# Routed experts of a mixture layer: weights copied to DRAM, fetched per slot by a register address, and used as the stationary operand

## The chip, the cores and the metric

The kernel runs on one core of one Trainium2 chip. The metric is device time in microseconds (us) of one execution. The kernel before has a median of 1341.43 us over 11 runs (1333.9 to 1348.31). One further execution was taken with the hardware profiler; all stage times and durations below come from it.

## The reference, cut to what matters

The model is one block with three residual layers over `x` of 2 x 2048 x 128, float32:

```python
x = x + 0.5 * ffn(layernorm(x))     # mixture of experts
x = x + attn(layernorm(x))          # a state-space (scan) layer
x = x + 0.5 * ffn(layernorm(x))     # the same mixture, same weights
```

The mixture, for each of the 4096 tokens (D = H = 128, E = 32 experts, 4 chosen of them, plus a shared expert of width 512):

```python
scores = softmax(flat @ router_w.T + router_bias)
topk_scores, topk_idx = top_k(scores, 4)              # then normalised to sum 1
h = silu(flat @ gate_w[e].T) * (flat @ up_w[e].T)     # for the chosen e
out = sum over chosen e of score_e * (h @ down_w[e].T)
out = out + (silu(flat @ sgate_w.T) * (flat @ sup_w.T)) @ sdown_w.T
```

The scan layer has 256 channels with 16 states each; the state runs along the 2048 positions of a sequence.

## The kernel before, in words

The 4096 tokens are eight blocks of 512 tokens (4 tiles of 128). A mixture layer treats blocks in groups: the first layer has groups (0,1), (2,3), (4,5,6,7), the second (0,1,2,3), (4,5), (6,7). For one group, `mixture` does this:

1. LayerNorm, transposition and routing (mostly VectorE). The routing gives each (token, expert) pair a row in a DRAM buffer in which every expert's rows start on a tile of 128, and a list `route["sl"]` of the expert that owns each tile, or *slot*. A group of two blocks has 64 slots, one of four has 96.
2. GpSimd (POOL) scatters the tokens to their rows by indirect DMA, 128 rows at a time (L924, one for each tile and each of the 4 choices). The buffer has been filled with zeros before by SyncE's DMAs (`clear_rows`, L480), since slots are padded: 16 transfers of 256 KB for a two-block group and 24 for a four-block group. The three buffers are reused by the second layer.
3. Four slots at a time (a *quad*; 224 / 4 = 56 a layer): SyncE loads the rows (L1014, tile `xs`), PE transposes them (L1023, `pt_x`), ACT copies them out of PSUM (L1026, `xT`); PE computes gate and up in one matmul per slot (L1040, `gu`), in which `xT` is the stationary operand and 256 columns of the expert's weights move; ACT takes the SiLU (L1059), VectorE multiplies (L1065, `h`); PE transposes `h` (L1023, `pt_h`), ACT copies it (L1073, `hT`); PE computes the down projection (L1078, `oq`), ACT copies it (L1087, `yq`), SyncE stores it (L1091).
4. When all quads of the group are stored, POOL gathers, for each tile, the 4 results of its tokens by indirect DMA (L1105, `yg`), and PE adds them with diagonal matrices of the scores (L1130, `sum`).

The shared expert (L958, L967, L973, L984) is done by block. All weights of the 32 routed and 4 shared pieces lie in SBUF, in `w_all`, 55 KB of each partition; `load_experts` fills it with 27 transfers of 256 KB (L449). The expert of a slot is chosen by a register: PE loads four entries of `route["sl"]` (L1032) and uses them as column offsets into `w_flat`:

```python
nc.tensor.matmul(gu.t[:, s, :], xT.t[:, s0 + s, :],
                 w_flat[:, bass.ds(offs["v"][s0 + s], 2 * H)], start=True, stop=True)
```

The scan layer (`state_space`) takes the blocks one after another. In each of 16 state steps of a block, SyncE broadcasts a row (L1344, `bs`), POOL multiplies (L1354, the *drive*), ACT makes the decays (L1366, `da`), VectorE scans two channel halves (L1392) and multiplies by C (L1405), PE transposes and adds (L1171). Before its 16 steps a block has a prologue (projection, softplus; POOL's part at L1322 to L1324).

Every engine executes its instructions in order. That order is written out by hand: the kernel first collects 4504 operations, and `ORDER` lists their numbers in the order of emission; an operation goes to the end of its engine's queue, SyncE's too, whose queue holds all loads and stores but the indirect ones. Buffers come from rings (`RINGS`: name and depth); an operation that writes a ring's buffer waits until all users of the buffer that had its place are done. Between successive indirect DMAs POOL sets a small tile (L414, `pad`) as a pause.

Of the kernel before, what the change touches and what calls it, by code (L numbers as in the profile page):

```python
# [8 lines left out]
F32 = mybir.dt.float32  # L9
# [4 lines left out]
ALU = mybir.AluOpType  # L14
# [3 lines left out]
P = 128  # L18
# [22 lines left out]
    shb=1, sg=2, hs=4, xs=3, xT=2, h=2, hT=2, yq=2, yg=2, dg=1,  # L41
    pro=1, u=1, z=1, xnTs=1, t2=4, dt=2, dtu=2, bs=3, cm=2, hst=4,
# [5 lines left out]
1 96 10 0 109 12 8 4-5 14 20 7 11 25 9 6 13 21 52 113 112 16 111 114-117 121-122 877 876 879 118-119 123-124 120  # L48
125-131 178 180 179 182-183 181 184-185 132 134 133 135-138 186-187 190 188-189 191-194 878 880 195 881 139 196-198
882 199 142 200 202 201 203-205 208 206 209 207 892 210 883 211 143 140 212 884 141 887 213 144-145 888-889 988-993  # L50
996 994-995 997 1000 998 1001 999 893 1002 894 1003 885 1004 39 18 26 22 17 24 19 15 98 27 29 28 23 40 46 34 2 94 3
73 79 72 93 85 35 48 32 104 59 31 45 44 63 110 88 82 77-78 49 102 494 56 92 84 886 1005 897 895-896 495 898-899 1006
1008 1007 1010-1011 1009 1012-1015 1018 1016 1019 1017 890 146 167 164 169 158 175 151 156 162 177 172-174 168 150
176 161 153 165 152 170 154 147-149 159 155 157 171 160 163 166 1020 900 1021-1022 496-497 891 901-902 498-499 903
1023 500 1024 1026 1025 1028-1030 904 906 1027 908 81 97 74-75 36 62 41 103 43 47 91 42 100 89 30 57 86 76 50 33 71
95 69 83 37 87 53 38 80 1031 905 907 909 108 214 90 105 228 242 70 51 68 215 442 216 106 66 256 1032-1033 1036 1034
1037 1035 1038-1039 910 912 1040 911 913-915 1041 217-220 229 221-223 230 224 243 916 244 231-232 225-226 233-235
257-258 917 236 245 237 246 238 247-248 259 249-250 260-261 239-240 270 64 58 61 227 241 60 67 284 65 298 251-252
262-264 560-562 271-272 253 563 920 265 254-255 266 273 276 285 274-275 277 286 267-268 278 921 279-280 287 290
# [263 lines left out]
def macaron_kernel(  # L323
# [110 lines left out]
    rb = load("rb", router_b.partition_broadcast(P), [P, E])  # L434


    w_all = const.tile([P, NE, 3 * H], F32, tag="w_all", name="w_all")
    w_flat = w_all.rearrange("p e f -> p (e f)")
    w_routed, w_shared = Buf(t=w_all), Buf(t=w_all)

# [1113 lines left out]
```

## Time and profile before

| | |
|---|---|
| median of 11 runs | 1341.43 us (1333.9 to 1348.31) |
| the profiled execution: its own time | 1337.09 us |
| its span, first to last instruction | 1335.3 us |
| mean granted TensorE clock | 0.921 |
| busy: PE / DVE / ACT / POOL | 1064.0 / 858.3 / 896.9 / 999.8 us |
| DMA traffic | 154.12 MB, mean 115 GB/s |

Milestones of that execution, by the starts of POOL's instructions: the first scatter at 28.0 us; the first scatter of the first layer's four-block group at 93.9; the first gather at 212.3; the first scan drive at 282.1; the last scan of block 3 ends at 596.5; the gathers of the four-block group from 588.2; the first drive of block 4 at 663.4; the last store of a quad at 1278.5; the last gather ends at 1327.2.

How to read it: busy time of an engine says little by itself, since each engine has to wait in its fixed order. What a change is worth in a stretch is read from the chain of work that ended last in that stretch, and from which engine's queue was never empty there. The chain's shares are in per cent of the stretch.

### The profile page before, as it was taken

The numbers are of one execution on the slowest core, as the hardware profiler recorded it, in microseconds if no ns is written. First come the engines' busy times: TensorE is split into PE (matmuls) and PEld (weight loads), VectorE is DVE, ScalarE is ACT, GpSimd is POOL, SyncE is SP. The second block draws the span as 40 slices with busy tenths as digits, with TensorE's granted clock in tenths as the row PEclk, the third lists the DMA queues.
The fourth block names the chain that finished last, engine by engine and source line by source line (L and its number), as shares of the span: only waits on it lengthen the run. The fifth ranks groups of instructions, "written<-read, shape, count | busy, mean of one in ns | idle before, by whom it ended". The sixth has DMA issues, their size and how long they took to land.

```text
span 1335.3 us, 19281 instructions
## 1 busy us (share of the span) xinstructions
PE 1064.0 (80%) x5842; PEld 804.3 (60%) x5842; DVE 858.3 (64%) x1567; ACT 896.9 (67%) x1704; POOL 999.8 (75%) x1108
## 2 busy tenths in 40 slices
PE   6899877878876887878776676788888888788875
PEld 3567556656655766766444453555667777567753
DVE  7576412279799998982599999998995434112211
ACT  4446333799897999976767576587986555456532
POOL 2838888887898546577888888896458468878776
PEclk9999998998997999996989787788999998989987
DMA  9955334444333425421122232222444433444432
GB/s 307 347 161 170 100 93 139 134 121 128 91 110 99 118 76 150 120 72 40 58 68 67 74 88 69 62 68 78 129 125 141 124 101 110 132 142 129 123 99 54
DMA packets 186726, 154.12 MB, mean 115 GB/s; under 512 B 17665, under 2 KB 154498, under 8 KB 186626
## 3 DMA queue, kind: packets, MB, share of 16 engines
q1 hardware_dynamic: 170242, 119.29, 30.6%
q0 software_dynamic: 16384, 33.59, 8.8%
q8 instruction: 51, 0.84, 0.3%
q14 instruction: 49, 0.40, 0.1%
HBM read 89.64 MB, written 63.18 MB: 114 GB/s over the span
## 4 chain that ended last, share of the span: by engine, by line
PE 31%; DVE 26%; POOL 16%; ACT 13%; issue 10%; DMA 2%; another core or an unknown queue 0%; POOLq 0%; DVEq 0%; SPq 0%; ACTq 0%
DVE hst L1392 12%; PE gu L1040 7%; POOL xs L924 6%; POOL yg L1105 5%; PE oq L1078 4%; DVE hst L1405 4%; POOL pad L414 4%; ACT L420 4%; PE sum L1130 3%; ACT da L1366 3%; PE pt_h L1023 2%; PE gp L958 2%; PE up L958 2%; PE pt_x L1023 2%; PE y L1171 2%
## 5 line engine op out<-in xcount | busy, mean ns | idle before, releaser
L1354 POOL TENSOR_TENSOR hst<-dtu,bs 128x1024 f32<-128x1024 f32 x128 | 302.9, 2376 | 122.6 <-ACT st L1417 33.6
L1105 POOL DMA_INDIRECT yg<-ys,idx x256 | 249.1, 973 | 101.6 <-issue 38.9
L1040 PE MATMUL gu<-w_all,xT 128*128 x896 | 240.9, 405 | 28.6 <-issue 13.1
L1392 DVE TENSOR_TENSOR_SCAN hst<-da,st,hst 128x512 f32<-128x512 f32 x192 | 237.8, 1269 | 13.4 <-ACT da L1366 9.3
L924 POOL DMA_INDIRECT xs<-xn,idx x192 | 189.1, 985 | 62.5 <-issue 33.2
L1065 DVE TENSOR_TENSOR h<-sgq,gu 128x256 f32<-128x256 f32 x224 | 89.5, 415 | 207.7 <-ACT sgq L1059 126.2
L1366 ACT ACTIVATE da<-dt,a 128x512 f32<-128x512 f32 x256 | 174.0, 691 | 60.5 <-DVE hst L1392 57.4
L1040 PEld LDWEIGHTS gu<-w_all,xT 128*128 128x128 f32 x896 | 165.9, 199 | 74.3 <-issue 26.0
L420 ACT ACT_TABLE_LOAD x148 | 189.9, 1283 | 3.4 <-PEq L1542 0.8
L1171 PEld LDWEIGHTS y<-ident,hst 128*128 128x128 f32 x1024 | 128.7, 151 | 69.2 <-issue 45.3
L1405 DVE TENSOR_TENSOR hst<-hst,c 128x1024 f32<-128x1024 f32 x128 | 156.1, 1220 | 12.7 <-PE c L1378 4.1
L1171 PE MATMUL y<-ident,hst 128*128 128x128 f32 x1024 | 141.8, 290 | 14.8 <-DVE hst L1405 11.6
L1078 PE MATMUL oq<-w_all,hT 128*128 x896 | 123.1, 282 | 13.1 <-ACT hT L1073 8.1
L414 POOL MEMSET pad<- 128x256 bf16 x402 | 132.3, 329 | 0.3
L1078 PEld LDWEIGHTS oq<-w_all,hT 128*128 128x128 f32 x896 | 113.3, 195 | 28.0 <-ACT hT L1073 13.0
L1059 ACT ACTIVATE sgq<-gu 128x256 f32<-128x256 f32 x224 | 81.7, 382 | 71.7 <-PE gu L1040 46.4
L1130 PE MATMUL sum<-yg,dg 128*128 128x128 f32 x512 | 85.3, 312 | 39.2 <-DMA yg<-ys,idx 26.3
L1122 ACT ACTIVATE dg<-ident,wk 128x128 f32<-128x128 f32 x256 | 81.5, 391 | 47.6 <-PE sum L1130 34.3
L1023 PE MATMUL pt_h<-ident,h 128*128 128x128 f32 x448 | 75.7, 289 | 45.1 <-DVE h L1065 30.0
L1130 PEld LDWEIGHTS sum<-yg,dg 128*128 128x128 f32 x512 | 75.9, 219 | 56.0 <-issue 32.3
L1087 ACT COPY yq<-oq 128x512 f32<-128x512 f32 x112 | 65.2, 584 | 63.9 <-PE pt_h L1023 18.0
L1378 PE MATMUL c<-cm,pick 128*128 128x512 bf16 x128 | 52.5, 410 | 58.4 <-DVE hst L1405 58.4
(151 smaller groups left out, 1720.1 us busy)
## 6 DMA issues: line engine op xcount, KB each, us to landing
bs<-bd SPq DMA_DIRECT2D x128, 256.0 KB
xs<-xs SPq DMA_DIRECT2D x112, 256.0 KB
ys<-yq SPq DMA_DIRECT2D x112, 256.0 KB
xs<-zero SPq DMA_DIRECT2D x56, 256.0 KB
yg<-ys,idx POOLq DMA_INDIRECT x256
xs<-xn,idx POOLq DMA_INDIRECT x192
x<-in_x SPq DMA_DIRECT2D x8, 256.0 KB
w_all<-in_up_w SPq DMA_DIRECT2D x8, 256.0 KB
```

Source lines behind the costliest of these rows:

```text
L414: pool(nc.gpsimd.memset(pad, 0.0))
L420: nc.scalar.preload_act_table_set(name)
L924: nc.gpsimd.indirect_dma_start(out=xs_b.t, out_offset=bass.IndirectOffsetOnAxis(ap=route["idx"][:, i * TB + t, k : k + 1], axis=0), in_=xn ...
L1040: nc.tensor.matmul(gu.t[:, s, :], xT.t[:, s0 + s, :], w_flat[:, bass.ds(offs["v"][s0 + s], 2 * H)], start=True, stop=True,)
L1078: nc.tensor.matmul(o.t[:, s, :], hT.t[:, s, :], w_flat[:, bass.ds(offs["v"][s] + 2 * H, D)], start=True, stop=True,)
L1105: nc.gpsimd.indirect_dma_start(out=yg.t[:, k, :], out_offset=None, in_=ys_b.t, in_offset=bass.IndirectOffsetOnAxis(ap=route["idx"][:, i * ...
L1130: nc.tensor.matmul(sm_.t, dg.t[:, k, :], yg.t[:, k, :], start=(k == 0), stop=(k == TOPK - 1),)
L1171: nc.tensor.matmul(y[:, t, k * P : (k + 1) * P], src[:, k, t * P : (t + 1) * P], ident.t, is_transpose=True, start=start and k == 0 and t ...
L1354: nc.gpsimd.tensor_tensor(h.t[:, :, 1:], dtu.t, bs.t.unsqueeze(1).to_broadcast([P, ND, T]), ALU.mult)
L1366: nc.scalar.activation(da.t, dt.t[:, k, :], AF.Exp, scale=a_t.t[:, k, s : s + 1])
L1392: nc.vector.tensor_tensor_scan(h.t[:, k, 1:], da.t, h.t[:, k, 1:], 0.0 if ini else st_sb[:, k, s : s + 1], ALU.mult, ALU.add,)
L1405: nc.vector.tensor_tensor(h.t[:, :, :T], h.t[:, :, 1:], cb.t.unsqueeze(1).to_broadcast([P, ND, T]), ALU.mult,)
```

## The change

- The routed experts' weights no longer lie in SBUF. `load_experts` copies them at the start from the three inputs into one DRAM tensor `w_dram` of [32 experts, 128, 384] (24 transfers of 256 KB, DRAM to DRAM). `w_all` keeps the four shared pieces alone.
- For every quad, SyncE loads the four owners from `route["sl"]` into registers and starts four transfers of 192 KB (128 rows of 1536 bytes), one for each slot, from `w_dram` at the register's address into a new ring `wt` (8 buffers of two slots). They stand in SyncE's queue among the other loads and stores. PE no longer loads registers.
- Gate and up become two matmuls per slot with the weights stationary and `xT` moving (128 columns), so that `gu` comes out with H on the partitions. `h` then has the layout that the down projection wants, and the transposition `pt_h` and the copy `hT` are gone. The down projection takes its moving operand from `wt`.
- Rings: `sg` 2 to 3, `xs` 3 to 4, `xT` and `h` 2 to 3, `yq` 2 to 3, `yg` 2 to 4, `dg` 1 to 2, `u`, `z` and `xnTs` 1 to 2.
- `ORDER` is another list of the same length. On a coarse scale (stages, scan blocks against groups) it is the old one; on a fine scale most operations have moved.

```diff
 RINGS = dict(
     y=1, da=2, c=1, w=3,
     xn=4, xnT=3, rt=1, lo=1, sc=1, mr=1, mk=1, cum=1, sm=1, route=3,
-    shb=1, sg=2, hs=4, xs=3, xT=2, h=2, hT=2, yq=2, yg=2, dg=1,
-    pro=1, u=1, z=1, xnTs=1, t2=4, dt=2, dtu=2, bs=3, cm=2, hst=4,
+    shb=1, sg=3, hs=4, xs=4, xT=3, h=3, wt=8, yq=3, yg=4, dg=2,
+    pro=1, u=2, z=2, xnTs=2, t2=4, dt=2, dtu=2, bs=3, cm=2, hst=4,
 )
...
-    w_all = const.tile([P, NE, 3 * H], F32, tag="w_all", name="w_all")
-    w_flat = w_all.rearrange("p e f -> p (e f)")
-    w_routed, w_shared = Buf(t=w_all), Buf(t=w_all)
+    w_all = const.tile([P, NSH, 3 * H], F32, tag="w_all", name="w_all")
+    w_shared, w_routed = Buf(t=w_all), dram_buf("w_dram", [E, P, 3 * H])

     def load_experts(c):
         for j, srcs in enumerate(((gate_w, sgate_w), (up_w, sup_w), (down_w, sdown_w))):
             shared = c == E // ECH
-            src = srcs[1] if shared else srcs[0][:, c * ECH : (c + 1) * ECH, :]
-            dst = w_all[:, c * ECH : (c + 1) * ECH, j * H : (j + 1) * H]
+            es, hs = slice(c * ECH, (c + 1) * ECH), slice(j * H, (j + 1) * H)
+            src = srcs[1] if shared else srcs[0][:, es, :].rearrange("p e h -> e p h")
+            dst = w_all[:, :, hs] if shared else w_routed.t[es, :, hs]
...
-            nc.vector.tensor_scalar(ej, ej, float(E - 1), 3.0 * H, ALU.min, ALU.mult)
+            nc.vector.tensor_scalar(ej, ej, float(E - 1), None, ALU.min)
...
+            wts = []
+            for s0 in range(0, SQ, 2):
+                wt = buf("wt", [P, 2, 3 * H])
+
+                def fetch(q=q, s0=s0, wt=wt, offs=offs):
+                    if s0 == 0:
+                        _, offs["v"] = nc.values_load_multi_w_load_instructions(
+                            route["sl"][0:1, q * SQ : (q + 1) * SQ],
+                            engines=[ET.SP],
...
+                    for s in range(2):
+                        nc.sync.dma_start(
+                            wt.t[:, s, :],
+                            w_routed.t[bass.ds(offs["v"][s0 + s], 1)].rearrange("e p f -> p (e f)"),
+                        )
+
+                op("sp", 1.6, fetch, r=[sl_b, route_b, w_routed], w=[wt, offs_b], size=4 * P * 2 * 3 * H)
+                wts.append(wt)
...
-                    for s in range(2):
-                        nc.tensor.matmul(
-                            gu.t[:, s, :],
-                            xT.t[:, s0 + s, :],
-                            w_flat[:, bass.ds(offs["v"][s0 + s], 2 * H)],
...
+                def gate_up(s0=s0, gu=gu, xT=xT, wt=wt):
+                    for j in range(2):
+                        for s in range(2):
+                            nc.tensor.matmul(
+                                gu.t[:, j, s, :],
+                                wt.t[:, s, j * H : (j + 1) * H],
+                                xT.t[:, s0 + s, :],
+                                start=True,
+                                stop=True,
+                            )
...
-            ph = buf("w", [P, SQ, P], name="pt_h")
-            op("pe", 0.45, lambda turn=turn, a=ph, b=h: turn(a, b), r=[h], w=[ph], hold=[hT])
-            op("act", 0.49, lambda a=hT, b=ph: nc.scalar.copy(a.t, b.t), r=[ph], w=[hT])
...
-                        hT.t[:, s, :],
-                        w_flat[:, bass.ds(offs["v"][s] + 2 * H, D)],
+                        h.t[:, s, :],
+                        wts[s // 2].t[:, s % 2, 2 * H :],
```

## The prediction

> **What bounds the kernel now.** I read the page first (busy times, slices, DMA), then the chain of waits cut into stretches, then the waits of POOL and the durations of the lines that the change touches. The busy times name no single bound, and the slices show DMA full only at the start:
>
> ```profile
> PE 1064.0 (80%) x5842; PEld 804.3 (60%) x5842; DVE 858.3 (64%) x1567; ACT 896.9 (67%) x1704; POOL 999.8 (75%) x1108
> DMA  9955334444333425421122232222444433444432
> q1 hardware_dynamic: 170242, 119.29, 30.6%
> ```
>
> The chain, cut at 28, 262, 600, 650, 1010 and 1280 us, has another owner in each stretch. These are the answers for 28 to 262, 650 to 1010, 1010 to 1280 and the end:
>
> ```profile
> by line: POOL xs L924 32.9%; POOL pad L414 14.1%; issue 9.9%; POOL yg L1105 8.2%; PE o L984 6.1%; PE gp L958 5.6%; PE up L958 4.6%; DMA yg<-ys,idx 3.9%; DVE hs L973 1.5%; PE pt_n L644 1.4%; PE lg L691 1.4%; DVE mr L744 1.1%; DVE x L996 1.1%
> by line: DVE hst L1392 25.2%; issue 10.6%; DVE hst L1405 8.5%; PE y L1171 3.1%; ACT L420 3.1%; ACT da L1366 2.8%; PE gp L958 2.8%; PE ps L1193 2.7%; PE up L958 2.3%; DVE hs L973 2.2%; DVE ea L1308 2.2%; PE gu L1040 1.7%; DVE bc L1255 1.5%;
> by line: PE gu L1040 28.5%; PE oq L1078 14.7%; PE sum L1130 9.3%; issue 9.2%; PE pt_h L1023 8.1%; PE pt_x L1023 7.0%; DVE h L1065 2.7%; ACT yq L1087 2.2%; PE ps_o L1475 1.9%; PE y L1171 1.8%; ACT dg L1122 1.8%; ACT sgq L1059 1.6%; another c
> by line: POOL yg L1105 50.8%; POOL pad L414 18.0%; issue 8.1%; DMA out_y<-x 4.9%; DMA yg<-ys,idx 4.5%; PE sum L1130 2.9%; POOLq L1550 1.9%; POOLq L1105 1.1%; DVE x L1141 0.5%
> ```
>
> So POOL's indirect DMAs set the time up to the first scan drive, VectorE (with ACT in 262 to 600, busy 307.87 of 338 us) that of the scans, PE that of the last mixture, and POOL's 32 last gathers the end. POOL's two long waits matter most here:
>
> ```profile
> 27.95 1.13 POOL L924 DMA_INDIRECT xs<-xn,idx  x1 [24.95 <-DMA w_all<-in_up_w]
> 93.92 0.96 POOL L924 DMA_INDIRECT xs<-dtu,idx  x1 [18.84 <-ACT sgq L1059]
> 95.38 0.96 POOL L924 DMA_INDIRECT xs<-dtu,idx  x1 [0.16 <-issue]
> ```
>
> The first scatter waits for its zeroed rows (DMA). At 93.92 POOL begins the four-block group, held by the routing. From there indirect DMAs follow each other every 1.455 us with nothing between, up to the first drive at 282.1: POOL has no slack, and a later start moves everything behind it.
>
> **Part 1, the start: the copy into `w_dram`.** Before, 27 weight loads share the queue with the zero fills, 68 us of it at 300 to 350 GB/s, and the first `xs` load is issued at 76.0. After, 24 of them are copies inside DRAM whose source is written expert by expert: the slowest dimension has 4 entries, the destination has 512 rows. What does a transfer with few outer entries do? The trace has one: `bout`, a single row. From section 6, the packets of q1 that carry data are 136705 of 512 B (`xs` and `ys` 224 x 512, `w_all` 27 x 512, `x` and `out` 16 x 512, `bout` 1), 23936 of 2 KB (`bs` and the fills 184 x 128, `win`, `wdt`, `bd` 384) and 1984 smaller, 162625 together. The line above counts 170242; the 7617 left are 476 x 16 + 1, for 477 transfers. [...]
>
> q1 took 30.6% of 16 x 1335.3 us for 119.29 MB, 55 ns per KB, 28 ns per 512 B. A copy of 512 rows is 512 x 28 / 16 = 0.9 us on sixteen engines, or 128 x 28 ns = 3.6 us on four; 24 of them 21.5 or 86 us. Ahead of or between them the same engines serve 43 fills and 11 loads of 256 KB (0.76 us each at the 347 GB/s of the second slice, 41 us) and the first 32 scatters (about 5 us). So `w_dram` is complete at about 2 + 41 + 5 + 21.5 = 70 us, or at 134 us. I take four, because the only row of a transfer with fewer than 16 outer entries used that many engines and no more.
>
> [...]
>
> Who waits? SyncE's queue is in order. In the new listing the first fetch, which needs the whole of `w_dram`, stands right behind these copies, and behind it the first `xs` loads and the last zero fill of the four-block buffer, with 14 fetches in front. That fill is issued about 10 us after `w_dram` is complete (14 fetches at 0.36 to 0.45 us, five register loads, some fills) and lands some 5 us later, behind 14 x 192 KB. The scatter of 93.92 then starts at about 150, 56 us late. From it to the first drive the old list has 121 indirect DMAs, the new one 114: 7 x 1.455 = 10 us less. Net +46 us. Bounds: with sixteen engines the fill lands at about 85 to 95, no delay, and -10 remains; with four engines and slower rows inside DRAM (a third more, 29 us) +75. PE's first quad moves from 80 to about 143, and needs 78 us of PE work until the 16th is stored; the first gather stands 69 DMAs, 100 us, behind the scatter, so this hides, with some 20 us to spare.
>
> **Part 2, the quad.** Removed on PE: four transpositions, 0.47 us a quad in steady rows; the register load and four offsets (0.33 + 4 x 0.04 us), of which only 'issue' gaps show, 13 + 26 us in all. Added: gate and up take 8 matmuls of 128 columns instead of 4 of 256. Rows: `gu` x8 takes 1.71 us (4 slots), `oq` x8, 128 columns, 0.97; so 1.94 instead of 1.71. Net -0.24 us for each of 112 quads, -27 us of PE work. On ACT `hT` goes, 112 x 0.585 = 65 us, and 8 of 148 table loads of 1.28. SiLU and product keep shape and duration, 0. POOL loses 22 of 402 pauses.
>
> Added to SyncE, a quad: one register load, four offsets, four transfers (0.36 to 0.45 us each): about 2.2 us, 245 us in all, beside some 200 of now 477 transfers. [...] `wt` waits make `bs`, `xs` and `ys` transfers wait behind them, and POOL and PE for those. DMA gains 448 x 192 KB, 88 MB: by 55 ns per KB 0.66 us of all engines each, 2.6 a quad.
>
> By stretch, against 1337.1 us:
> - 262 to 600, 32 quads: ACT loses 19 us of 308, and about 30% of this chain is ACT; PE's `pt_h` and ACT's `hT` are 10 us of it. -12 (0 to -25).
> - 600 to 650: the new list puts 51 gathers instead of 42 before block 4's first drive: +13 (0 to +13). They are missing later among the drives of blocks 4 to 6, where VectorE is as near to the bound as POOL: -6 (0 to -13).
> - Last block, with `u`, `z`, `xnTs` doubled so that a prologue can go ahead: -5 (0 to -15); what is late next is VectorE, 337 of 360 us busy.
> - From the last scan to the last store, PE: the list has 164.5 us of PE work there before, 149.7 after, and the register gaps (8 us there): -17 (-35 to +10). Next is POOL, about 188 us of DMAs in the 255.
> - The 32 last gathers: 0.
> - SyncE's order and a fuller DMA queue: +5 (0 to +40), near the low end since `xs` waits cost PE 8.6 us in the whole run.
>
> Sum: 46 - 12 + 13 - 6 - 5 - 17 + 5 = +24, so 1361 us beside the profiled execution's 1337.1, which lies 0.32% under the median of 1341.43. For a median that is 1365 us.
>
> **The rivals.**
> - *Wide copy, faster.* The copies run on 16 engines. Place: the wait at 93.92. Then part 1 is -10 and the sum -32: 1305, as a median 1309. It decides from where the copy takes under some 1.3 us (no delay at all) and breaks even near 2.7 us (`w_dram` at about 113). For it: every transfer but one in the trace is wide. Against: the one that isn't.
> - *Queue behind the fetch.* The delay as forecast, and SyncE's waits for a `wt` buffer hold up `bs` loads and stores in the later stretches too; with +40 instead of +5, 1396, as a median 1400. For it: SyncE already waits 332 us for POOL's drives in front of `bs`; against: it is mostly early.
> - *Delay eaten.* As forecast at the start, but ACT and PE relief count fully (-25, -35, -13, -15, no gather cost): about 1295 + 46 = 1341 or less, no change.
> - That rings are deeper without effect where the list doesn't use them is part of the ranges above.
>
> **How the numbers follow.** Forecast 0.58, wide copy 0.15, queue 0.13, eaten 0.14. About 0.3% (4 us) is what a measurement here can tell from no change. Faster: 0.14 of the wide copy, 0.08 of the eaten delay, 0.03 of the forecast, 0.25. Same: 0.01 + 0.03 + 0.05 = 0.09. Slower: 0.66. The forecast's own range is 1340 to 1390. The 8-in-10 range reaches to the wide copy's 1309 with 6 us below, and to the queue's 1400: 1303 to 1402.
>
> **What would show it.** Right: DMA's slices fall to about a quarter (4 of 16 engines) before some 135 us, POOL's wait before the first `xs<-dtu` scatter grows from 18.8 to about 70 us and is ended by a fill, PE idles there, the first drive is near 328; the PE stretch before the last store is shorter by some 15 us; `pt_h` and `hT` rows are gone. Wrong: a first scatter of that group before 100 us (wide copy), or a first drive near 328 and a total beyond 1390 with SyncE's waits at `wt` ahead of `bs` (queue).

## The result and the profile after

The changed kernel takes 1396.13 us (median of 16 runs, 1389.31 to 1400.34), the kernel before 1339.5 us beside it (62 runs). The ratio is 1.0429, 95% interval 1.0411 to 1.0447: 57 us slower. The profiled execution took 1396.81 us, with a span of 1395.0 and a mean granted clock of 0.88.

The page of the kernel after, its lines for PE, the DMA slices and the first queue:

```profile
PE 1043.2 (75%) x6290; PEld 837.5 (60%) x6290; DVE 853.5 (61%) x1567; ACT 828.1 (59%) x1584; POOL 992.2 (71%) x1086
...
DMA  8547766876673567683112223224498867778841
...
q1 hardware_dynamic: 234466, 207.40, 48.8%
```

PE's busy time fell by 21 us (1064.0 to 1043.2), although it now runs 448 instructions more. The first queue carries 207.40 MB instead of 119.29. DMA's slices mostly stand at 5 to 8 where they were 2 to 5, in the first half of the span and again from the 29th slice on; in the ten slices between, the later scan blocks, they are 1 to 4 in both.

The windows view cuts both spans at the first scan drive and at the end of the last one. Its columns are the stretch, its length in us, busy us and count of PE, PEld, DVE, ACT and POOL, the clock, DMA's share and GB/s. Before:

```profile
0.00:282.10 282.10, 232.50 (x1204) 166.29 (x1205) 127.36 (x448) 141.76 (x284) 210.36 (x328) 0.97 0.57 176
282.10:1024.60 742.50, 582.38 (x3170) 435.72 (x3168) 646.57 (x878) 597.87 (x1056) 559.27 (x422) 0.90 0.33 93
1024.60:1335.30 310.70, 249.11 (x1471) 202.26 (x1470) 84.34 (x243) 157.32 (x365) 230.22 (x358) 0.93 0.41 114
```

After:

```profile
0.00:342.30 342.30, 242.55 (x1311) 183.82 (x1312) 124.52 (x444) 126.86 (x258) 198.63 (x313) 0.85 0.66 208
342.30:1087.00 744.70, 569.51 (x3436) 450.79 (x3436) 652.90 (x897) 576.16 (x1021) 587.25 (x453) 0.89 0.49 147
1087.00:1395.00 308.00, 231.09 (x1547) 202.91 (x1546) 76.09 (x228) 125.05 (x306) 206.29 (x321) 0.89 0.68 201
```

The first stretch grew by 60 us (282.1 to 342.3), the scans by 2 us, the last stretch shrank by 3. The whole loss lies ahead of the first drive. The scans and the last mixture have gained next to nothing.

The chain of waits after, for 28 to 342, 710 to 1065 and 1087 to 1338 (views cut short on the right by their width):

```profile
by line: issue 17.5%; PE gu L1061 11.0%; PE o L984 8.2%; PE oq L1089 6.9%; PE gp L958 6.3%; SPq L480 6.3%; PE up L958 6.1%; PE pt_x L1051 4.3%; SPq L449 3.8%; DVE h L1079 2.4%; PE lg L691 2.2%; DMA w_dram<-in_up_w 2.0%; PE sum L1141 1.8%; a
...
by line: DVE hst L1403 25.1%; ACT L419 9.2%; issue 8.5%; DVE hst L1416 6.5%; ACT da L1377 5.6%; PE y L1182 4.7%; PE o L984 2.7%; ACT sg L967 1.8%; PE ps_o L1486 1.7%; DVE ea L1319 1.5%; DVE hs L973 1.5%; DVE bc L1266 1.5%; POOL hst L1365 1.
...
by line: PE gu L1061 23.5%; issue 21.0%; PE oq L1089 14.6%; PE sum L1141 9.9%; PE pt_x L1051 8.0%; another core or an unknown queue 3.5%; DVE h L1079 2.9%; ACT sgq L1073 1.6%; ACT xT L1054 1.6%; PE ps_o L1486 1.5%; PE lg L691 1.5%; ACT xn L
```

At the start POOL's scatters (32.9% of 28 to 262 before) no longer own the chain: 'issue', PE's quads (`gu`, `oq`) and PE's shared expert (`o`, `gp`, `up`) do. The scans belong to VectorE as before. In the last mixture `pt_h` and `hT` are gone, but 'issue', time in which the engine waited for nothing that the profile shows, is 21.0% of 251 us, 53 us, where it was 9.2% of 270 us, 25 us. What was taken off PE did not come out of the stretch. The end is POOL's gathers as before (`yg` 45.0%, `pad` 16.0%).

POOL's five longest waits between 76 us and the first drive (POOL's timeline; start, duration, instruction, in brackets the idle time and its releaser):

```profile
141.92 0.96 POOL L924 DMA_INDIRECT xs<-dtu,idx  x1 [63.93 <-DMA wt<-w_dram]
...
197.85 0.96 POOL L924 DMA_INDIRECT xs<-xn,idx  x1 [12.21 <-DVE h L1079]
...
259.16 0.98 POOL L1116 DMA_INDIRECT yg<-ys,idx  x1 [4.71 <-DMA wt<-w_dram]
...
291.06 0.96 POOL L1116 DMA_INDIRECT yg<-ys,idx  x1 [2.75 <-PE sum L1141]
...
332.83 1.26 POOL L1333 TENSOR_TENSOR w<-w,ea 128x512 f32<-128x512 f32 x1 [7.05 <-ACT w L1328]
```

The wait of 18.84 us before the four-block group's first scatter became one of 63.93 us. Four more follow, 26.7 us together, the last of them before the scan's prologue; the kernel before has one of 1.22 us there.

**Who held the scatter at 141.92?** The releaser named there, a fetch, had nothing to do with its data. The timelines of PE, VectorE and SyncE give the answer. After:

```profile
130.41 1.09 PE L1051 MATMUL pt_x<-ident,xs 128*128 128x128 f32 x4 [34.83 <-DMA xs<-xs]
131.29 0.63 PE L769 MATMUL tot<-mk,ones 128*128 128x512 bf16 x1
```

```profile
91.75 1.25 DVE L757 TENSOR_SCALAR mk<-mr 128x512 bf16<-128x512 f32 x1
...
131.97 1.22 DVE L777 TENSOR_TENSOR_SCAN cum<-one,tot 128x512 f32<-128x512 f32 x1 [35.59 <-PE tot L769]
...
140.98 0.20 DVE L855 TENSOR_SCALAR idx<-p 128x64 uint32<-128x64 f32 x1
```

```profile
122.27 3.35 SPq L1033 DMA_DIRECT2D wt<-w_dram  x6
125.71 0.39 SPq L1014 DMA_DIRECT2D xs<-xs  x1
```

Before, PE and VectorE at the same place:

```profile
79.27 0.63 PE L1023 MATMUL pt_x<-ident,xs 128*128 128x128 f32 x4 [0.17 <-DMA xs<-xs]
```

```profile
84.04 1.21 DVE L777 TENSOR_TENSOR_SCAN cum<-one,tot 128x512 f32<-128x512 f32 x1
```

The scatter needs `idx`, the routing, which VectorE finished at 141.18. That chain begins with PE's matmul `tot` (L769). Its operand `mk` was ready at 93.00, 38 us before it ran; but in PE's queue `tot` stands right behind `pt_x`, the transposition of the first quad's rows, and PE idled 34.83 us until those rows came. Their load stands in SyncE's queue behind six fetches (issued from 122.27), which need the whole of `w_dram`. In the old list, too, `tot` comes behind the first `pt_x`, but there the rows were in time. From `cum` (L777) to the scatter it takes 9.95 us here and 9.88 before (84.04 to 93.92): only the beginning moved, by 47.9 us. In each of the 20 traces of this case the scatter starts 0.94 or 0.95 us after `idx` does.

### The profile page after: what moved, and what is told of

Its sections match the earlier page's. It is cut to its first block, busy times and chain, and to the rows that moved or that the text cites. A ratio compares the mean times of both kernels' runs of the same rounds, so it can differ in the third digit from the quotient of the medians.

```text
span 1395.0 us, 20723 instructions
## 1 busy us (share of the span) xinstructions
PE 1043.2 (75%) x6290; PEld 837.5 (60%) x6290; DVE 853.5 (61%) x1567; ACT 828.1 (59%) x1584; POOL 992.2 (71%) x1086
## 2 busy tenths in 40 slices
DMA packets 250961, 242.32 MB, mean 174 GB/s; under 512 B 24545, under 2 KB 218722, under 8 KB 250850
## 3 DMA queue, kind: packets, MB, share of 16 engines
q1 hardware_dynamic: 234466, 207.40, 48.8%
## 4 chain that ended last, share of the span: by engine, by line
PE 36%; DVE 27%; issue 14%; ACT 12%; POOL 5%; SPq 3%; DMA 2%; another core or an unknown queue 1%; POOLq 0%; DVEq 0%; ACTq 0%
DVE hst L1403 12%; PE gu L1061 8%; PE oq L1089 6%; ACT L419 3%; DVE hst L1416 3%; PE y L1182 3%; PE sum L1141 3%; PE pt_x L1051 3%; PE o L984 3%; POOL yg L1116 2%; ACT da L1377 2%; PE gp L958 2%; DVE h L1079 2%; PE up L958 2%; SPq L480 2%
## 5 line engine op out<-in xcount | busy, mean ns | idle before, releaser
L1061 PE MATMUL gu<-xT,wt 128*128 128x128 f32 x1792 | 248.8, 292 | 51.0 <-issue 21.1
L1061 PEld LDWEIGHTS gu<-xT,wt 128*128 128x128 f32 x1792 | 230.5, 204 | 78.8 <-issue 32.6
L1089 PE MATMUL oq<-wt,h 128*128 128x128 f32 x896 | 141.4, 308 | 43.6 <-DVE h L1079 26.6
L1089 PEld LDWEIGHTS oq<-wt,h 128*128 128x128 f32 x896 | 127.7, 218 | 56.4 <-DVE h L1079 31.8
L413 POOL MEMSET pad<- 128x256 bf16 x380 | 124.6, 328 | 0.2
L1051 PE MATMUL pt_x<-ident,xs 128*128 128x128 f32 x448 | 74.8, 299 | 65.6 <-DMA xs<-xs 38.8
L1054 ACT COPY xT<-pt_x 128x512 f32<-128x512 f32 x112 | 64.5, 584 | 90.6 <-PE pt_x L1051 66.1
L924 POOL DMA_INDIRECT xs<-dtu,idx x64 | 62.7, 979 | 75.4 <-DMA wt<-w_dram 63.9
L1051 PEld LDWEIGHTS pt_x<-ident,xs 128*128 128x128 f32 x448 | 57.4, 154 | 80.2 <-issue 62.4
L1141 PE MATMUL sum<-yg,dg 128*128 128x128 f32 x512 | 82.0, 313 | 29.8 <-DMA yg<-ys,idx 16.4
```

Source lines behind the costliest of these rows:

```text
L413: pool(nc.gpsimd.memset(pad, 0.0))
L924: nc.gpsimd.indirect_dma_start(out=xs_b.t, out_offset=bass.IndirectOffsetOnAxis(ap=route["idx"][:, i * TB + t, k : k + 1], axis=0), in_=xn ...
L1051: nc.tensor.transpose(dst_.t[:, s, :], src_.t[:, s, :], ident.t)
L1061: nc.tensor.matmul(gu.t[:, j, s, :], wt.t[:, s, j * H : (j + 1) * H], xT.t[:, s0 + s, :], start=True, stop=True,)
L1089: nc.tensor.matmul(o.t[:, s, :], h.t[:, s, :], wts[s // 2].t[:, s % 2, 2 * H :], start=True, stop=True,)
```

## Experiments

Times differ between occasions: the kernel before took 1397.5 us beside the first four runs below, 1338.5 to 1344.9 beside most others and 1321.9 once. So each run is read as its ratio to the kernel before on the same chip at the same time; stretches are from each run's profiled execution, cut as above. "Start" is the time of the first drive, "last" what follows the last drive.

### The copy: how wide, and whether at all

**The copy row by row.** The outer dimension of source and destination has 128 entries; nothing else differs.

```diff
-            src = srcs[1] if shared else srcs[0][:, es, :].rearrange("p e h -> e p h")
-            dst = w_all[:, :, hs] if shared else w_routed.t[es, :, hs]
+            src = srcs[1] if shared else srcs[0][:, es, :]
+            dst = w_all[:, :, hs] if shared else w_routed.t[es, :, hs].rearrange("e p h -> p e h")
```

> The changed kernel with one edit: the 24 copies into w_dram are written row by row on both sides (128 outer entries) instead of expert by expert (4). Same bytes, same queue, same order. Theory N (the narrow copy is the loss): w_dram is complete near 70 to 75 us, the first xs<-dtu scatter is at 85 to 100 us instead of 141.9, the first drive at 275 to 290 instead of 342.3, and as the two kernels take the same time from the first drive to the end (1052.7 and 1053.2 us) the total is 1330 to 1345. Theory Q (SyncE's order is the loss: fills and xs loads stand behind fetches, however fast the copy): the scatter stays beyond 110 us, total 1360 to 1385. Theory T (fetch traffic costs the later stages and the early delay was partly hidden): first drive near 282, but more than 1060 us from it to the end, total 1350 or more.

Measured: 1.0216 (1.0139 to 1.0294), the four-block scatter at 109.7, the first drive at 338.4. Less is lost than with the narrow copy, but neither scatter nor drive came as early as the first theory had them.

**No copy.** The weights come packed, as one input; `load_experts` loads the shared pieces alone.

```diff
...
-    w_shared, w_routed = Buf(t=w_all), dram_buf("w_dram", [E, P, 3 * H])
+    w_shared, w_routed = Buf(t=w_all), Buf(t=experts)
...
```

> The changed kernel without the copy: the host hands the experts' weights over already packed expert by expert (an arrangement of the same values), the fetches read that input, and the 24 copies are gone from SyncE and the DMA queue. Theory N: at least as early as the wide copy, by 0 to 20 us: scatter at 75 to 95 us, first drive 265 to 285, total 1320 to 1340. Theory Q: the scatter waits for the routing that the first fetch needs, and stays beyond 105 us, total 1355 to 1380. Theory T: first drive at 282 or before and still a total of 1345 or more.

Measured: 1.0101 (1.0031 to 1.0170), scatter at 99.1, first drive at 321.2, again later than expected.

**Zero fills first.** Nine fills of the four-block buffer move ahead of the first fetch in `ORDER`; the narrow copy stays.

> The changed kernel, narrow copy kept, with the nine zero fills that stood behind the first fetch on SyncE moved in front of it. Theory Q: the wait for the fill was the loss: scatter of the four-block group at 95 to 105 us, first drive at 290 to 300, total 1345 to 1355. Theory N with a second hold (the first quads start only when w_dram is complete near 120 us, and the in-order queues of VectorE and PE put them ahead of later routing): the scatter comes at about 95 to 105 us, but POOL waits later, for the routing and for the first ys rows, the first drive stays at 325 to 342, total 1378 to 1396.

Measured: 1.0495 (1.0405 to 1.0586), scatter at 147.1; both theories had it at 95 to 105. The fills were not what it waited for. Up to them the two SyncE queues agree within 0.5 us, though the chips differ: the last group of fills starts at 116.53 after and at 117.01 here. Behind it the first `xs` load is issued at 131.74 instead of 125.71, since the nine fills now stand ahead of it, and VectorE's timeline has the routing as much later:

```profile
131.74 0.39 SPq L1022 DMA_DIRECT2D xs<-xs  x1
```

```profile
137.40 1.22 DVE L785 TENSOR_TENSOR_SCAN cum<-one,tot 128x512 f32<-128x512 f32 x1 [33.38 <-PE tot L777]
...
146.17 0.20 DVE L863 TENSOR_SCALAR idx<-p 128x64 uint32<-128x64 f32 x1
```

Load +6.0, `cum` +5.4, `idx` +5.2, scatter +5.2 us: the chain through `pt_x` and `tot` carries the delay.

**Twelve copies of eight experts.** Each has eight outer entries.

```diff
+            whole = shared or c % 2
+            if not shared:
+                es = slice((c - 1) * ECH, (c + 1) * ECH)
+                src = srcs[0][:, es, :].rearrange("p e h -> e p h") if whole else None
+                dst = w_routed.t[es, :, hs] if whole else None
...
```

> The changed kernel with 12 copies of 8 experts instead of 24 of 4, still expert by expert: 8 outer entries, the same bytes and rows. Theory N (a copy is spread over as many engines as it has outer entries): in stretches with nothing but copies DMA is busy on 8 of 16 engines (0.5 to 0.58, against 0.29), w_dram is complete at 85 to 95 us, the scatter at 105 to 118, total 1350 to 1368. If the number of outer entries doesn't set the spread (rows inside DRAM are slow by themselves): no change, 1390 to 1400.

Measured: 1.0183 (1.0114 to 1.0251), scatter at 108.5, like the wide copy. In both PE no longer waits for the first rows (`pt_x` starts at 98.12 and 99.24 without a wait), but the routing's `mk` itself is late (it starts at 94.45 and 95.57, in the kernel before at 81.66); no run tells why.

How many engines a copy uses is seen in ten microseconds of the DMA view, in 40 slices (busy tenths, GB/s). After, 85 to 95 us:

```profile
DMA  3223222222222239999953222222222399722222
GB/s 115 61 61 74 82 86 88 86 86 88 86 88 84 88 121 365 383 365 381 385 182 100 92 104 98 98 102 92 82 88 86 119 377 379 260 86 88 88 92 92
```

With eight outer entries, 60 to 70 us:

```profile
DMA  8655459555568579999999996754596334489996
GB/s 313 244 197 207 184 191 311 172 184 172 182 199 270 186 230 350 371 379 369 365 408 340 397 377 254 279 229 178 186 305 150 86 104 121 137 268 313 340 342 149
```

Between the fills' bursts (9 tenths, 365 to 383 GB/s), the copies with four outer entries run mostly at 2 tenths and 82 to 92 GB/s, as four of sixteen engines would. With eight it is mostly 4 to 6 tenths and 172 to 207 GB/s.

**The same again on other chips,** the changed kernel, its wide copy and no copy:

> The changed kernel as it is, so that the following variants have it beside them on their chip. All theories: ratio 1.035 to 1.06 to the kernel before, TensorE's granted clock below that of the kernel before, and ACT starting its SiLU over 1.2 us late behind the last recorded gate/up weight load some 30 times.

> The changed kernel itself, beside them. Late completions: 1.038 to 1.046. None: the start keeps its 45 us of narrow copy, the last stretch falls to 265 to 275 us, 0.98 to 1.00.

> The changed kernel with the wide copy, a second time, beside the others on one chip. If only the copy's bytes are left to pay: 5 to 20 us at the start behind the kernel without the copy, the two later stretches as there, ratio 1.01 to 1.022. If the wide copy left nothing to pay: equal to the kernel without the copy within 0.003.

> The changed kernel without the copy, a second time, beside the half above on one chip. With a third of each fetch it had 293, 741 and 308 us. Theory P: 293 to 298, 741 to 745, 308 to 312, ratio 1.002 to 1.007. Theory F: 305 or more at the start, 320 or more at the end, ratio 1.015 or more.

Measured: changed 1.0410 (1.0356 to 1.0464) and 1.0413 (1.0371 to 1.0455), wide 1.0186 (1.0127 to 1.0246), no copy 1.0091 (1.0051 to 1.0130). First drives at 341.9, 345.6, 309.9 and 296.4. By the first, third and fourth the narrowness costs 32 us and a wide copy another 13.5 (its bytes and its issues weren't separated), and these 45.5 us lie at the start. Without any copy the kernel is still slower, by 0.9%.

### Which operand stands still

**Rows held.** No copy, and gate and up as one matmul of 256 columns for each slot, with `xT` stationary; `h` goes on without its transposition.

```diff
...
-                    for j in range(2):
-                        for s in range(2):
-                            nc.tensor.matmul(
-                                gu.t[:, j, s, :],
-                                wt.t[:, s, j * H : (j + 1) * H],
-                                xT.t[:, s0 + s, :],
...
+                    for s in range(2):
+                        nc.tensor.matmul(
+                            gu.t[:, s, :, :].rearrange("p j h -> p (j h)"),
+                            xT.t[:, s0 + s, :],
+                            wt.t[:, s, 0 : 2 * H],
...
```

> The changed kernel without the copy (packed input) and with the rows held in TensorE again: gate and up in 4 matmuls of 256 columns a quad, fetched weights moving, 8 records instead of 16. It leaves out the transposition of h, which this orientation would need, so it has the smallest TensorE work of all. Theory P: ratio 0.96 to 0.99 where the same kernel with the weights held had 1.010; SiLUs hardly ever late. Theory F: the fetches are unchanged, 1.00 to 1.012.

Measured: 0.9799 (0.9757 to 0.9841). Against no copy with the weights held (1.0091, on another chip) the difference is which operand stands still, and with it four matmuls of 256 columns for eight of 128; it is worth 2.9%, 39 us. The windows, weights held and then rows held:

```profile
0.00:296.40 296.40, 235.70 (x1311) 177.64 (x1312) 124.35 (x444) 126.87 (x258) 198.92 (x314) 0.93 0.70 219
296.40:1036.90 740.50, 562.20 (x3435) 442.98 (x3434) 647.63 (x897) 576.08 (x1021) 586.13 (x453) 0.90 0.50 147
1036.90:1348.20 311.30, 234.76 (x1549) 205.53 (x1547) 77.30 (x229) 125.62 (x306) 206.46 (x321) 0.88 0.68 199
```

```profile
0.00:279.30 279.30, 228.40 (x1103) 163.18 (x1104) 124.05 (x444) 126.84 (x258) 198.89 (x314) 0.93 0.74 232
279.30:1021.40 742.10, 564.45 (x3085) 429.48 (x3084) 650.71 (x897) 579.93 (x1027) 585.99 (x453) 0.90 0.50 148
1021.40:1309.70 288.30, 218.07 (x1208) 178.74 (x1208) 75.70 (x227) 120.87 (x301) 205.99 (x320) 0.90 0.71 213
```

PE's busy time differs by 22 us in all (1032.7 and 1010.9), by 7.3 at the start and 16.7 in the last stretch; the stretches differ by 17.1 and 23.0. At the start POOL waits, behind the four-block group's first scatter, 27.6 us (9.60, 8.94, 2.56 and 6.47) with the weights held and 10.4 us (5.10, 2.48 and 2.79) with the rows held: for the routing of group (2,3), for stored quads and before the prologue. The 17.2 us between the sums are the whole difference of the two starts.

**The split alone, in the old kernel.** Each matmul of 256 columns in two of 128; order, transpositions, weights in SBUF and the stationary rows are before's.

```diff
                     for s in range(2):
-                        nc.tensor.matmul(
-                            gu.t[:, s, :],
-                            xT.t[:, s0 + s, :],
-                            w_flat[:, bass.ds(offs["v"][s0 + s], 2 * H)],
...
+                        for j in range(2):
+                            nc.tensor.matmul(
+                                gu.t[:, s, j * H : (j + 1) * H],
+                                xT.t[:, s0 + s, :],
+                                w_flat[:, bass.ds(offs["v"][s0 + s] + j * H, H)],
...
```

> The kernel before with one edit: each gate/up matmul of 256 columns is written as two of 128 (16 records and 16 weight loads a quad instead of 8), as many as in the changed kernel; four more register additions a quad on TensorE, all else as before. Theory P (many narrow matmuls, each with a weight load of its own, cost TensorE more than the spacing of their rows shows, and its completions come late): 25 to 60 us more, ratio 1.02 to 1.045, SiLUs late over 1.2 us 20 times or more. Theory F (fetch traffic and SyncE's order cost the later stages): no fetches here, so the rows' 0.2 us a quad plus 0.15 us of registers, at most 10 us where TensorE is the bound, ratio 0.998 to 1.008.

Measured: 1.0257 (1.0210 to 1.0304); start 298.8 (+17), last 329.6 (+19). It has four register additions a quad besides, so this is an upper bound for the split. That it lands beside the 2.9% suggests that the count of matmuls costs this, whichever operand stands still. The granted clock does not explain it: this run's is 0.920, that of the kernel before 0.921.

**Is it the stream itself?** Behind the end of the no-copy kernel, six streams of gate-and-up matmuls in turns, the same work narrow and wide, each closed by a VectorE copy; fetches run beside the first two and part of the third.

> The disputed cost by itself. The changed kernel without the copy, and behind its end six streams on TensorE, each fenced by a copy on VectorE that waits for its last matmul: fp32 with the shared experts' weights, 64 matmuls of 256 columns (128 records) and 128 of 128 columns (256 records), alone; both again beside 64 fetches of 192 KB on SyncE; both again alone. The output is untouched by them. By the spacing of the rows (0.214 and 0.112 us a record) the two streams take 27.4 and 28.7 us, the narrow one 5% more. Theory P in the form 'a weight load is not hidden under 128 columns': wide 27 to 30, narrow 36 to 50 us, 30% more or over. If the streams come out as their rows say, the loss of the narrow form lies in the waits between TensorE, ACT and VectorE and not in the stream. Theory F in the form 'fetches slow TensorE itself': the streams beside the fetches take 10% more or over; otherwise within 3%.

Measured (one execution; VectorE's timeline, idle time in brackets is the length of a stream: narrow, wide, narrow; then windows in a narrow stream with fetches and in a narrow one without):

```profile
1394.33 0.29 DVE L1558 COPY burst<-burst 128x128 f32<-128x128 f32 x1 [28.29 <-PE burst L1524]
1421.96 0.29 DVE L1558 COPY burst<-burst 128x128 f32<-128x128 f32 x1 [27.34 <-PE burst L1524]
1450.54 0.29 DVE L1558 COPY burst<-burst 128x128 f32<-128x128 f32 x1 [28.29 <-PE burst L1524]
```

```profile
1366.00:1394.00 28.00, 28.00 (x253) 28.00 (x252) 0.04 (x1) 0.00 (x0) 0.00 (x0) 1.00 1.03 356
1423.00:1450.00 27.00, 27.00 (x244) 27.00 (x243) 0.00 (x0) 0.00 (x0) 0.00 (x0) 1.00 0.01 1
```

28.29 us narrow, 27.34 wide: 3.5%, about what the rows' spacing says (5%), and far from 30%. A stream is the work of 16 quads, so this is 0.06 us a quad. At 356 GB/s beside it the narrow stream takes what it takes alone. Neither the stream's length nor the fetches' traffic explains 39 us.

**One matmul more for each half quad,** with rows held, and with weights held (the lines shown):

```diff
+                    nc.tensor.matmul(
+                        gu.t[:, 0, 0, :], wt.t[:, 0, :H], xT.t[:, s0, :], start=True, stop=True
+                    )
```

> How much time does known TensorE work cost here? The kernel without the copy and with the rows held (ratio 0.980; it leaves out the transposition of h), plus one repeated matmul of 128 columns in each gate/up pair, two a quad: by the measured stream 2 x 0.221 = 0.44 us a quad, 33 us on the some 75 quads of the first and last stretch. If TensorE work there is paid once: 279 to 295, 742, 289 to 308 us, ratio 1.000 to 1.010. If it is paid more than once, because ACT and VectorE answer later and the next quad waits for them: 305 or more at the start or 318 or more at the end, ratio 1.015 or more. If it is hidden: 0.980 to 0.990, and the loss of the narrow form (0.980 to 1.009) has nothing to do with its length.

> The same two extra matmuls a quad in the changed kernel without the copy (weights held, ratio 1.009; 296, 741 and 311 us). Paid once: 1.030 to 1.038. Paid more than once: 1.045 or more. Hidden: 1.009 to 1.018.

> The changed kernel without the copy, beside the next two on one chip. In the two runs with extra matmuls TensorE's completions came with the ends of its rows (0 us late in all), where in every run before them they came late by 250 to 400 us in sum, and the kernel before took 1322 us instead of 1340 to 1345. If that is the chip's condition at the time and not the extra matmuls: with late completions again (the kernel before at 1335 us or more) ratio 1.004 to 1.014; without them (before at 1325 or less) 0.94 to 0.965. If the extra matmuls themselves took the lateness away: 1.004 to 1.014 while the next kernel stays at 0.96 to 0.975.

> The same with two extra matmuls a quad, a second time. If the chip's condition decided: 0 to 0.04 above the kernel without them, so 1.03 or more where completions are late and 0.965 to 0.975 where they are not. If the extra matmuls are the cause: 0.96 to 0.975 either way.

Measured: 0.9662 (0.9617 to 0.9707) and 0.9680 (0.9634 to 0.9727), both on one occasion on which the kernel before took 1321.9 us; on another, no copy 1.0106 (1.0053 to 1.0160) and the weights held with one more 1.0231 (1.0198 to 1.0265). The same kernel gave 0.968 and 1.023. The first two lie below all that was expected of them, and 1.0231 below the 1.03 expected where completions are late. On the second occasion the added work, two matmuls a quad of two records each at 0.112 us, 0.45 us, comes to 29 us on the 65 quads outside the scans (26 before the first drive, 39 behind the last), and cost 18 us (1355.6 to 1373.5). So added PE work isn't paid more than once, which speaks against a toll on each matmul. The first occasion's chip has the same number as that of the run with the rows held, 26 minutes earlier, where the kernel before took 1344.9 us. On the first occasion the orientation cost nothing, and the last mixture's chain had other owners, POOL and DMA, with 'issue' at 5.3% (the kernel with weights held and one more, 1016.6 to 1223):

```profile
by line: POOL yg L1118 19.4%; PE gu L1063 13.1%; PE oq L1091 7.7%; DMA wt<-in_experts 7.4%; DMA yg<-ys,idx 7.3%; DMA xs<-xs 7.0%; POOL pad L411 6.8%; issue 5.3%; PE pt_x L1050 3.5%; PE gu L1058 3.5%; PE sum L1143 3.3%; ACT xn L627 1.4%; DVE
```

### The fetches

**A third of the bytes.** No copy; each fetch brings 64 KB, and gate's weights serve for up and down too.

> The changed kernel without the copy and with a third of each fetch: only the 128 gate columns of an expert are fetched (64 KB instead of 192), and its gate weights stand in for its up and down weights in the same matmuls. Same instructions, 59 MB less traffic. Theory F: ratio 0.97 to 0.995 instead of 1.010. Theory P: within 0.005 of 1.010.

Measured: 1.0018 (0.9988 to 1.0047), against 1.0091 with the whole fetch: two thirds of the bytes are worth 0.7%, 10 us (6 us between the profiled spans); that lies between the two theories. The two were taken on different chips.

**Fetches in the old order.** The kernel before with its order, rows held and transpositions, but weights fetched from the packed input (ring of 7 quads); each fetch stands as early in SyncE's queue as the ring lets it. The second run fetches 64 KB, gate's weights serving for up and down.

> One half of the change alone: the kernel before, its order, its rings and its orientation (rows held, 256 columns, transposition of h) kept, but the weights fetched by register-addressed transfers from packed input (no copy), a quad's four fetches on SyncE right behind its xs load, ring of 7 quads; no register loads on TensorE. Stretches to compare, in us: start to first drive, first drive to last, last drive to end: 282, 743, 311 in the kernel before. Theory P (the narrow matmuls are the loss, the fetches are not): 265 to 285, 740 to 745, 298 to 310, ratio 0.98 to 1.00. Theory F (the fetches' traffic and SyncE's place in the order are a loss of their own): last stretch 318 or more, ratio 1.005 to 1.03.

> The half above (the kernel before with fetched weights, ratio 1.030: 296, 758 and 327 us) with a third of each fetch: 64 KB of an expert's gate columns, which stand in for its up and down weights; matmuls of the same number and width. Theory F in the form 'bytes': 283 to 288, 743 to 748, 312 to 318, ratio 1.000 to 1.012. Theory F in the form 'issue and order on SyncE' (a register load and four transfers behind every xs load, in an order made without them): within 0.006 of 1.030.

Measured: 1.0302 (1.0241 to 1.0362) with 192 KB, 1.0237 (1.0159 to 1.0315) with 64 KB. Start 296.1 (+14), scans 758.0 (+15), last 327.3 (+17). The difference between the two lies within their intervals, so most of this loss isn't bytes; what is left, by elimination and not by a run of its own, is the register reads and four issues a quad, in a SyncE queue whose order was made without them. In the new order with the same fetches the scans take 740.5 us, which speaks for the new list and its rings.

Rows held is below both kernels, but without the transposition that it would need. With it, in the new order, it wasn't tried. Of the complete versions none is below the kernel before, except on that one occasion.

## Why the prediction was wrong

The direction was right (slower) and the time inside the range, but +24 us were forecast and +57 measured. By its terms:

| term | forecast | measured |
|---|---|---|
| four-block scatter | at 150, +56 | at 141.9, +48 |
| from that scatter to the first drive | -10 | 188.2 to 200.4, +12 |
| scans, prologues | -12 +13 -6 -5 = -10 | 742.5 to 744.7, +2 |
| last mixture and gathers | -17 | 310.7 to 308.0, -3 |
| SyncE's order, fuller DMA | +5 | within the rows above; +6 to +10 for two thirds of the bytes |

Two steps failed: what the scatter waits for, and what the narrow matmuls of a quad cost. Against the forecast the scatter comes 8 us earlier, but the way from it to the first drive is 22 us longer, the scans are 12 us longer and the last mixture with the gathers 14.

- *Four engines: right.* 24 copies at 3.6 us were the forecast, and the DMA view of 85 to 95 us shows the quarter (the page's slices, with the fills in them, don't). SyncE reaches the first fetch's issue at 122.27 (forecast: `w_dram` complete at 134). With a wide copy the forecast's bound was no delay; the scatter came at 109.7 and 111.2, not at 93.9. That the 16 and the 1 of its packet count stand for engines was the forecast's own estimate, and no run shows what these packets are. Their number came out at four for a copy: the page after has 6880 packets under 512 B more than the page before (24545 and 17665), which is 16 for each of the 448 fetches less 12 for each of the 24 copies. And between the fills the DMA was busy mostly at 2 tenths with four outer entries and at 4 to 6 with eight, near 4 and 8 of 16 engines.
- *"Who waits?": the first step that failed.* The prediction let the scatter wait for the last zero fill behind 14 fetches. It waited for the routing, whose `tot` stands behind the first quad's `pt_x` on PE (48 us later than before). Moving the fills forward made it 5.2 us later, not earlier. That 150 came near 142 is luck: the last fills and the first `xs` load stand close together behind the same fetches. The prediction had PE idle until 143 at the first quad and did not ask what else was queued behind that instruction.
- *"This hides, with some 20 us to spare": failed.* Behind the scatter POOL did save 11 us of work by the shorter list (166.3 to 154.9 us busy up to the first drive, forecast -10), but it idled 24 us more (21.9 to 45.5). The first of these waits, 12.21 us at 197.85, again ends 0.7 us after a routing (`idx` of group (2,3), written at 196.93 to 197.11); the next two stand before gathers, the last (7.05 us) before the prologue. With the rows held the same way from scatter to drive takes 185.2 us (94.1 to 279.3), -3 instead of the forecast's -10; with the weights held 201.6 (94.8 to 296.4). So the failure here is mostly that of the next point.
- *"1.94 instead of 1.71", "net -0.24 us" for a quad: the term that was mis-sized.* By twice the row of `oq` x8 the eight narrow matmuls cost 0.23 us a quad more, 26 us of PE work, of which some 15 lie outside the scans; in an unbroken stream it was 0.06 us a quad. That work is there (PE busy 22 us more than with the rows held), but the time is 39 us, +17 at the start and +23 in the last stretch. Rows held, with the transpositions gone, the last stretch is 288.3 us, -22: the forecast's mechanism, PE relieved of `pt_h` and of register gaps, exists and would have given -17 and more, but here without the transposition that this orientation needs. The narrow form takes it back.
- *Why 39 and not 15 stays open in part.* Shown: not stream length, not fetch traffic, not PE work paid several times. Shown too: PE's results reached the next engine later than its rows ended. Of the 224 SiLUs, those that begin over 1.2 us after the last weight load of their `gu` has ended, with ACT idle as long, are 2 in the kernel before, 32 after, 30 with no copy, 16 with the rows held (hardly any were expected), 27 in the old kernel with the split, 5 in the old kernel with fetches, and 2 each in the two kernels that took 0.968 and 0.966. The first of these two had 47 on the second occasion: the same kernel, so the occasion decides whether they are late at all; where they are, the narrow form has the most. A lower clock is not the reason: of the 32, 28 lie clear of the stretches in which the trace has the granted clock at 0.50. Where `oq` stands soon behind `gu`, PE waits for `h`. The no-copy kernel with weights held (PE's timeline, group (0,1)):

```profile
113.87 2.94 PE L1060 MATMUL gu<-xT,wt 128*128 128x128 f32 x24 [0.82 <-issue]
117.80 1.16 PE L1088 MATMUL oq<-wt,h 128*128 128x128 f32 x8 [0.99 <-DVE h L1078]
119.97 0.66 PE L1050 MATMUL pt_x<-ident,xs 128*128 128x128 f32 x4 [1.01 <-DVE h L1078]
```

and with rows held, at the same place in the list:

```profile
109.60 2.86 PE L1059 MATMUL gu<-wt,xT 128*128 128x256 f32 x12
112.30 1.05 PE L1087 MATMUL oq<-wt,h 128*128 128x128 f32 x8
113.19 0.60 PE L1050 MATMUL pt_x<-ident,xs 128*128 128x128 f32 x4
```

There `oq` begins 1 us after 24 narrow `gu` have ended, waiting for `h`, and `pt_x` waits again; with 12 wide `gu` it follows at once. What makes completions late, and why they were timely on one occasion, no run settles. Whether the changed kernel would lose less on such an occasion wasn't run.
- *Scans: failed as a gain.* ACT's 65 us and the deeper rings bought nothing: 742.5 before, 740 to 751 in every variant of the new order, 746 in the old one with the split. By the chain the stretch is VectorE's.
- *Rivals.* Wide copy: false. "Queue behind the fetch" gave 1400, next to the 1396 measured, by a mechanism that isn't there: the scans, where `bs` loads would have been held, kept their length. In the old order, though, fetches did cost +15 us in the scans. Delay eaten: false; its sum was also wrong, since 1337.1 - 25 - 35 - 13 - 15 + 46 is 1295 and not 1341, so by its own terms this rival stood for a faster kernel.

## What to carry to other kernels

When a load gets later, list everything queued behind its first consumer on that engine, not only the data that the next stage names: here a routing matmul behind one waiting transposition moved a whole group's scatters by 48 us. Look at how many outer entries a copy has: eight did here what 128 did (ratios of 1.0183, and of 1.0216 and 1.0186), four cost some 32 us. Fewer, wider matmuls were worth more than their rows say in two comparisons (2.6 and 2.9%) and nothing on one other occasion, for a reason that stays open; in the last mixture holding the weights took back (23 us) what the missing transpositions and register loads had brought (22 us).

## What the runs showed of the hardware

- *Behind a narrow copy the issuing queue was held up too, 3.2 to 3.4 us at a time.* SyncE's timeline after; the duration is the issue's own:

```profile
67.17 3.24 SPq L480 DMA_DIRECT2D xs<-zero  x1
70.46 0.65 SPq L449 DMA_DIRECT2D w_dram<-in_down_w  x1
71.15 3.37 SPq L480 DMA_DIRECT2D xs<-zero  x1
74.56 0.66 SPq L449 DMA_DIRECT2D w_dram<-in_down_w  x1
```

A fill behind a narrow copy takes 3.2 to 3.4 us to issue here, where one takes 0.42 at 32.55 us in the kernel before. SyncE went at some 4 us for a copy and a fill (70.46 to 74.56), and everything behind on its list with it: it reached the first fetch at 122.27 with four outer entries, at 88.38 with eight and at 71.72 with 128 (the last two on another chip).
- *PE's completion lagged, here by 7.4 us.* In the kernel after, the shared expert's `o` ends by its rows (their ends are modelled) at 68.35, and the add that needs it starts at 75.77, at a granted clock of 1.00 from 68 to 74; in the kernel with one more matmul and weights held, 62.72 and 62.75 at the same place (PE's and VectorE's timelines):

```profile
61.60 6.75 PE L984 MATMUL o<-w_all,hs 128*128 128x128 f32 x32 [2.53 <-issue]
```

```profile
75.77 0.69 DVE L996 SCALAR_TENSOR_TENSOR x<-o,x 128x512 f32<-128x512 f32 x1 [9.74 <-remote]
```

```profile
58.98 3.74 PE L983 MATMUL o<-w_all,hs 128*128 128x128 f32 x32
```

```profile
62.75 0.69 DVE L995 SCALAR_TENSOR_TENSOR x<-o,x 128x512 f32<-128x512 f32 x1 [1.85 <-PE o L983]
```

- *PE came out of its idle time at a lower clock:* behind the 34.83 us in which it waited for the first rows, `pt_x` takes 1.09 us at a granted clock of 0.50, and the same four take 0.60 eight us later at 1.00. The start's mean granted clock is 0.85 after and 0.97 before.
- *PE's stream didn't feel the DMA:* 28.29 us with 356 GB/s beside it, 28.29 us with 1 GB/s.
